# Layer 0 of a two-layer convolution kernel: large transfers cut into parts that are issued in successive groups

## The chip, the cores and the metric

The kernel runs on one core of a Trainium2 chip. The metric is the time of one execution on the device in microseconds (us). Engines are named as in the profile: PE (matrix multiplications; PEld is its loading of weights), DVE, ACT and POOL (vector, activation and general engine), and SP, which here only issues transfers (DMAs). ACT and POOL can issue transfers too.

## The reference

The input x has 4 images of 16 channels and 256 x 256 pixels. Two layers follow each other; each adds to x a function of the group-normalized x (8 groups of 2 channels).

```python
# layer 0: 25 logits per channel from a 3x3 convolution, softmax over them,
# weighted sum of the 5x5 neighbourhood of the normalized input
out = conv3x3(gn(x), conv_w) + conv_b              # 16 * 25 outputs per pixel
weights = softmax(out.reshape(N, C, 25, H, W), axis=2)
x = x + einsum('ncuij,ncuij->ncij', unfold5x5(gn(x)), weights)
# layer 1: silu and 8 cubic B-spline bases of each 3x3 patch, two small contractions
out = einsum('bjhwn,ijn->bihw', silu(patches), base_w)
out = out + einsum('bjhwns,ijns->bihw', bspl, spl_w) + bias
x = x + out
```

## The kernel before

A short start computes the statistics of x and prepares the weights. Then `layer0` computes the first layer, and `layer1` the second; layer 1 begins when layer 0's last strips are done.

**Strips and groups.** Layer 0 goes over 64 strips: 4 images (`b`), 2 halves of 128 rows (`hf`, the rows lie on the partitions), 8 strips of 32 columns (`s`). A strip has 8 groups of `JG` = 4 columns, so layer 0 has 512 groups. For one group PE multiplies, for each of the 4 columns, a piece of the tile `am` (L922) and of the tile `an` (L926) with the weights, which gives the 400 logits `lg` (in PSUM, three buffers). ACT takes their exponential into `e` (L945, two instructions per group, four buffers of `e`). POOL multiplies `e` with the 5x5 neighbourhood `u` (L950). DVE sums numerator and denominator into `nd` (L771). At the end of a strip ACT and DVE divide (L785 to L799), and POOL subtracts the result from the columns of `xc` (L805).

**What is loaded.** The tiles `am` and `an` hold the transposed columns of the normalized input for 8 columns, two groups, from the arrays `hst` and `hsl` in HBM. `load_im` issues three DMAs for `am` (L719) and two for `an` (L729), 779 KB together, two such periods ahead, into three buffers. `load_u` issues five DMAs of 288 KB (L743) for the next strip in the middle of a strip (column 16). `load_xc` issues one of 1 MB (L749), every fourth strip, for the four strips that come two strips later: `xc` holds 128 columns of x for all 16 channels. When the four strips have been subtracted, `xc` is x1, the result of layer 0, and `store` (L862) writes it twice into the array `x1s` for layer 1: two DMAs of 1 MB, issued by ACT, 15 times. The last one, the sixteenth, is issued by POOL.

**The next image.** While an image is computed, the generator `normalize` prepares the next one, one step per group: it loads rows `xp` (L315), ACT normalizes them into `hsp` and `ht`, `hsp` is stored (`put_rows`, L323), PE transposes `ht`, ACT copies the result into `tt` and `hi` (L393), DVE computes the remainder `lo` (L414), and `put_columns` (L337) stores the three tiles for both halves: six DMAs of 260 KB. The list `moves` holds what is due after a number of groups.

**What sets the order.** The program is written out as one sequence, and `in_order` makes each engine keep the order of that sequence. Within a group the sequence is: `load_im` (every second group), `load_u` and `load_xc` (at column 16), the matrix multiplications and exponentials, POOL's product, DVE's sum of the group before, then `step()`, then one step of `normalize`. `after(k, f)` puts `f` in the list `later`; `step()` runs what is due and counts the rest down, so `f` comes in the k-th group after. POOL's subtraction calls `after(1 + g, statistics, ...)` for the eight channel groups g and `after(2, store, n, xc)`; the store thus comes in group 0 of the strip two further than the last of the four.

SP, ACT and POOL each issue their transfers in their own order. The framework adds the waits: a transfer waits for the buffer it fills to be free, for the data it reads, and, since it announces its landing through one of a small number of semaphores that are used in turn, for the transfer that used that semaphore before. The turn runs through the transfers of SP and ACT together.

Of the kernel before, what the change touches and what calls it, by code (L numbers as in the profile page):

```python
# [34 lines left out]
def conv_preact_kernel(  # L35
# [12 lines left out]
    nc = tc.nc  # L48
    B, C, H, W = x.shape
    G = 8  # L50
    GC = C // G
    P = 128
    NH = H // P
    K = 5
# [7 lines left out]
    SW = 32  # L62
# [3 lines left out]
    CX = 128  # L66
# [4 lines left out]
    QC = 4  # L71
# [36 lines left out]
    for k, d in enumerate((0, RD - 1)):  # L108
        h = k * (P // 2)
# [148 lines left out]
    def zeros(b, queue):  # L258

        for e in (0, HP - PAD):  # L260
            for r in range(PAD):
                yield partial(
                    queue.dma_start,
                    hs[b][:, e + r].rearrange("s c w -> c s w"),
                    zero[0:C, 0 : NST * SP].rearrange("c (s w) -> c s w", s=NST),
                )
        yield partial(
            queue.dma_start,
            bass.AP(
                tensor=x1s[b].tensor, offset=x1s[b].offset,  # L270
                ap=[[CP, C], [(H + 1) * W, 2], [1, W]],
            ),
            zero[0 : 2 * C, 0:W],
        )
        for h in range(NH):
            for w in (0, (W + 1) * RP):
                yield partial(queue.dma_start, hst[b][h][:, w : w + RP], zero[0:C, 0:RP])
                yield partial(
                    queue.dma_start,
                    hsl[b][h][:, :, w : w + RP].rearrange("c t r -> (c t) r"), zero[:, 0:RP],  # L280
                )
# [8 lines left out]
    def normalize(b, ptr, tiles, held=None, copier=None, part=None, dense=False):  # L290
# [5 lines left out]
        prep, xps, tts, his, los = tiles  # L296
        copier = copier or nc.scalar.copy

        moves = [(20 + 4 * i, f) for i, f in enumerate(zeros(b, nc.sync))]
        moves = moves if held is None and part is None else []  # L300
# [25 lines left out]
                hsp.rearrange("p s c w -> p s (c w)"),  # L326
            )

        def put_columns(q, n):
            g0 = n * QG  # L330
            for h in parts:

                for to, ti, t in ((hst, 0, tts[n]), (hsl, 0, his[n]), (hsl, 1, los[n])):
                    d = to[b][h]
                    m = 2 if to is hsl else 1
                    t = t if t.dtype == F32 else t.bitcast(F32)
                    nc.sync.dma_start(  # L337
                        bass.AP(
                            tensor=d.tensor,
                            offset=d.offset + q * QC * m * CT + ti * CT + (1 + g0) * RP,  # L340
                            ap=[[QW * RP, W // QW], [m * CT, QC], [1, QG * RP]],
                        ),
                        t[:, h].rearrange("p g r -> p (g r)"),
                    )
# [41 lines left out]
        def columns(q, n, h):  # L386

            tp = ptr.tile([P, QG, P], F32, name=f"tp{b}_{q}_{n}_{h}", tag="tp")

            def copy(t, to, keep):  # L390

                if h in parts:
                    to(t[:, h, :, 1 : 1 + P], tp)  # L393
                if part == 1:
                    to(t[:, 1, :, 0:1], keep[:, q * NQ + n])
                elif h == 1:
                    to(t[:, 0, :, RP - 1 :], tp[:, :, 0:1])
                else:
                    to(t[:, 1, :, 0:1] if part is None else keep[:, q * NQ + n], tp[:, :, P - 1 :])

            for k in range(QG):
                nc.tensor.transpose(
                    tp[:, k, :], hts[q, h][:, n * QG + k].rearrange("p w c -> p (w c)"), ident
                )
            if not dense:
                yield
            copy(tts[n], copier, kept[0])
            copy(his[n], nc.scalar.copy, kept[1])
            if not dense:
                yield  # L410

            v = slice(1, 1 + P) if h in parts else slice(RP - 1, RP)
            to = h if h in parts else 0
            nc.vector.tensor_sub(  # L414
                los[n][:, to, :, v], tp[:, :, 0 : v.stop - v.start],
                his[n][:, to, :, v].bitcast(F32),
            )
            if part == 0 and h == 0:
                moves.append((1, partial(
                    nc.scalar.copy, kept[2][:, q * NQ + n], los[n][:, 0, :, P : P + 1]  # L420
                )))
            if part == 1:
                nc.scalar.copy(los[n][:, 1, :, 0:1], kept[2][:, q * NQ + n])
            if h == NH - 1:
                if part is None:
                    moves.append((5, partial(border, los[n])))
                moves.append((9 if part is None else 4, partial(put_columns, q, n)))
            yield
            yield
            yield  # L430
            yield
# [28 lines left out]
    with tc.tile_pool(name="prep0", bufs=2) as prep, tc.tile_pool(  # L460
# [24 lines left out]
        for dj in range(3):  # L485
            v = conv_wt[dj].rearrange("(d c) n -> c d n", d=3)
# [5 lines left out]
        v = conv_wt[2, 2 * C : 3 * C]  # L492
# [10 lines left out]
        for d in range(3):  # L503
# [3 lines left out]
            v = spl_s[dc]  # L507
# [89 lines left out]
        for b in range(B):  # L597
            st = stat.tile([P, G, NH * (GC if b == 0 else 1), 6], F32, name=f"st0_{b}", tag=f"st0{min(b, 1)}")
            for hf in range(NH):
                n = b * NH + hf  # L600
                t = loaded.pop(0)
# [27 lines left out]
            ms = stat.tile([P, 2], F32, name=f"ms_{b}", tag="ms")  # L629
# [5 lines left out]
            v = hm[:, b * NH : (b + 1) * NH]  # L635
# [46 lines left out]
    def newest(engine):  # L682
        return [i for i in nc.cur_bb.bb.instructions if i.engine == engine][-1]
# [7 lines left out]
    def layer0(shift):  # L691
# [4 lines left out]
        with tc.tile_pool(name=f"prep{arm}", bufs=2) as prep, tc.tile_pool(  # L696
# [38 lines left out]
                    )  # L735
                return am, an

            def load_u(n):
                b, hf, s = strips[n]
                u = l0.tile([P, K, C, SP], F32, name=f"u_{n}{arm}", tag="u")  # L740
                for m in range(K):
                    r0 = hf * P + m
                    nc.sync.dma_start(u[:, m], hs[b][s, r0 : r0 + P])  # L743
                return u

            def load_xc(n):
                b, hf, s = strips[n]
                xc = x1p.tile([P, C, CX], F32, name=f"xc_{n}{arm}", tag="xc")
                nc.sync.dma_start(  # L749
                    xc, x[b, :, hf * P : (hf + 1) * P, s * SW : s * SW + CX].rearrange(  # L750
                        "c p w -> p c w")
                )
                return xc

            waiting, later, seeds = [], [], []

            def after(k, f, *args):

                later.append([k, partial(f, *args)])
# [36 lines left out]
            def quotient(n, nd, xc, r):  # L798
                nc.vector.tensor_mul(nd[:, 1], nd[:, 1], r)  # L799
                after(LAG + 2, apply, n, nd, xc)  # L800

            def apply(n, nd, xc):
                w0 = strips[n][2] * SW % CX
                v = xc[:, :, w0 : w0 + SW]
                nc.gpsimd.tensor_sub(v, v, nd[:, 1])  # L805
                seeds[1:] = [newest(POOLE)]
                if w0 + SW == CX:
                    if n == len(strips) - 1:
                        store(n, xc)
                        after(1, last_statistics, n, xc)  # L810
                    else:
                        for g in range(G):
                            after(1 + g, statistics, n, xc, g)
                        after(2, store, n, xc)

            def columns_of(n):
                b, hf, s = strips[n]
# [34 lines left out]
                add(vz, vz, mz)  # L852
                nc.gpsimd.tensor_scalar(st1[b][:, 1, :, k], vz, float(GC * CX), None, ALU.mult)

            def store(n, xc):
                b, hf, s = strips[n]
                c0 = s * SW + SW - CX
                v = x1s[b][:, W : W + H * W].rearrange("c (p w) -> p c w", w=W)

                queue = nc.gpsimd if n == len(strips) - 1 else nc.scalar  # L860
                for h in range(2):
                    queue.dma_start(  # L862
                        v[hf * P : (hf + 1) * P, h * C : (h + 1) * C, c0 : c0 + CX], xc
                    )


            nc.scalar.add_instruction(
# [5 lines left out]
                )  # L873
            )
            ims = [load_im(0)]
            us = [load_u(0)]
            ims.append(load_im(1))
            nxc, xc = load_xc(0), None
            ahead = iter(())
            for n, (b, hf, s) in enumerate(strips):  # L880
                if (hf, s) == (0, 0):
# [17 lines left out]
                u = us.pop(0)  # L899
                if s * SW % CX == 0:  # L900
                    xc = nxc

                nd = ndp.tile([P, 2, C, SW], F32, name=f"nd_{n}{arm}", tag="nd")
                for j in range(0, SW, JG):
                    if j % CI == 0:
                        k = n * nci + j // CI
# [5 lines left out]
                    if j == SW // 2:  # L912
                        if n + 1 < len(strips):
                            us.append(load_u(n + 1))
                        if s * SW % CX == 2 * SW and n + 2 < len(strips):
                            nxc = load_xc(n + 2)
                    e = l0.tile([P, 2, JG, K, C, K], F32, name=f"e_{n}_{j}{arm}", tag="e", bufs=LAG + 3)
                    for j1 in range(0, JG, 2):
# [12 lines left out]
                        if shift:  # L931
                            mx = l0.tile([P, 2, C], F32, name=f"mx_{n}_{j}_{j1}{arm}", tag="mx")
                            for i in range(2):
                                v = lg[:, i, :NL].rearrange("p (m c d) -> p m c d", m=K, c=C)
# [404 lines left out]
    with tc.If(fast > 0) as small_logits:  # L1339
        layer1("", *layer0(False))  # L1340
# [44 lines left out]
```

## Time and profile before

| | |
|---|---|
| median of 3 runs | 2912.49 us (2910.01 to 2913.32) |
| the profiled execution | 2906.7 us, its span 2904.9 us |
| busy share of the span: PE, DVE, ACT, POOL | 93%, 96%, 73%, 93% |
| moved by the DMAs | 664.43 MB, mean 229 GB/s |
| layer 0, first to last L771 | 123.8 to 2028.5 us |
| L950 on POOL, L771 on DVE, mean of one | 3.547 us, 3.477 us |

A row of the profile names line, engine, operation, and tiles as out<-in; then, after the bar, busy us in total and mean ns of one; then the idle time of the engine just before such instructions and which instruction's end ended it. Back-to-back instructions overlap by about 0.08 us. A row with SPq or ACTq is of the engine's issuing part: the second number is the time of issuing, not of the transfer. A view of waits has, for each pair, the total us, how many waits, and the longest.

### The profile page before, as it was taken

What the parts mean: (1) busy time and instruction counts of PE and PEld (TensorE: products, weight loads), DVE (VectorE), ACT (ScalarE), POOL (GpSimd) and SP (SyncE); (2) the same over time, 40 slices, a digit from 0 to 9 for tenths busy, and PEclk for the clock granted to TensorE, in tenths of its full rate; (3) what the DMA queues carried; (4) which work ended last, traced back from release to release, by engine and by line L of the source; (5) the groups of instructions that cost most, each with busy time, mean ns of one, the idle gap of its engine ahead of it and who ended that gap; (6) DMA issues with size and microseconds to landing.
All of it is one profiled execution on the core that took longest, in us unless ns stands there. A gap on an engine that the chain in (4) does not pass through costs nothing.

```text
span 2904.9 us, 40991 instructions
## 1 busy us (share of the span) xinstructions
PE 2715.8 (93%) x14282; PEld 1499.0 (52%) x14282; DVE 2803.1 (96%) x1866; ACT 2126.4 (73%) x2764; POOL 2704.7 (93%) x1117
## 2 busy tenths in 40 slices
PE   4699999999999999999999999997799999999998
PEld 3466656666666656656656656664233343333222
DVE  7599999999999999999999999999899999999996
ACT  6566876667757567676655655557899999999995
POOL 4399999999999999999999999999899999999995
PEclk7799999999999999999999999999899999999999
DMA  9988999879889688888976767765788888787883
GB/s 284 263 236 233 253 257 268 238 212 248 237 229 259 190 223 232 236 245 229 249 205 178 189 168 196 186 177 177 248 250 251 250 248 257 239 265 241 254 250 100
DMA packets 403467, 664.43 MB, mean 229 GB/s; under 512 B 43186, under 2 KB 267908, under 8 KB 387380
## 3 DMA queue, kind: packets, MB, share of 16 engines
q1 hardware_dynamic: 339284, 626.53, 76.5%
q10 hardware_dynamic: 61920, 31.46, 3.8%
q0 software_dynamic: 2048, 3.72, 0.4%
q8 instruction: 117, 1.92, 0.3%
q14 instruction: 98, 0.80, 0.1%
HBM read 532.96 MB, written 121.15 MB: 225 GB/s over the span
## 4 chain that ended last, share of the span: by engine, by line
DVE 49%; PE 27%; DMA 7%; ACT 6%; issue 5%; POOL 3%; SPq 2%; DVEq 0%; ACTq 0%; POOLq 0%
DVE nd L771 39%; PE yp L1252 12%; PE lg L922 10%; PE yp L1261 3%; PE lg L926 3%; DVE ring L175 3%; DVE s L172 2%; DMA an<-hsl 2%; POOL e L950 2%; DMA x1s<-xc 1%; DMA xin<-in_x_dram 1%; DVE r1a L1096 1%; ACT xtb L1087 1%; DVE nd L799 1%; DVE r L795 1%
## 5 line engine op out<-in xcount | busy, mean ns | idle before, releaser
L950 POOL TENSOR_TENSOR e<-e,u 128x1600 f32<-128x1600 f32 x512 | 1789.0, 3547 | 48.9 <-ACT e L945 32.4
L922 PE MATMUL lg<-wm,am 128*128 128x400 f32 x4096 | 1736.9, 505 | 69.8 <-ACT e L945 37.5
L771 DVE TENSOR_REDUCE nd<-e 128x128 f32<-128x3200 f32 x512 | 1758.6, 3477 | 29.7 <-POOL e L950 29.3
L926 PE MATMUL lg<-wn,an 97*128 97x400 f32 x2048 | 1346.9, 658 | 15.2 <-DMA an<-hsl 15.2
L945 ACT ACTIVATE e<-lg 128x800 f32<-128x800 f32 x1024 | 835.3, 839 | 578.2 <-PE lg L926 337.8
L922 PEld LDWEIGHTS lg<-wm,am 128*128 128x128 f32 x4096 | 764.9, 193 | 383.0 <-ACT e L945 69.1
L1252 PE MATMUL yp<-ring,wt 128*32 128x512 f32 x6144 | 722.2, 595 | 35.4 <-DVE ring L175 34.8
L926 PEld LDWEIGHTS lg<-wn,an 97*128 97x128 f32 x2048 | 389.0, 190 | 334.3 <-DMA an<-hsl 23.6
L1252 PEld LDWEIGHTS yp<-ring,wt 128*32 128x32 f32 x6144 | 228.8, 109 | 494.5 <-issue 404.3
L1109 POOL TENSOR_TENSOR s1b<-s1b,r1a 128x1024 f32<-128x1024 f32 (+1 forms) x96 | 192.7, 2038 | 0.0
L1109 POOL TENSOR_TENSOR s1a<-s1a,r1a 128x1024 f32<-128x1024 f32 (+1 forms) x96 | 192.0, 2031 | 0.0
L825 ACT ACTIVATE z<-xc,nrm 128x256 f32<-128x256 f32 x240 | 144.0, 600 | 17.5 <-POOL xc L805 13.5
L175 DVE SCALAR_TENSOR_TENSOR ring<-s,s1a 128x1024 f32<-128x1024 f32 x132 | 154.9, 1193 | 0.9
L175 DVE SCALAR_TENSOR_TENSOR ring<-s,s1b 128x1024 f32<-128x1024 f32 (+1 forms) x128 | 152.0, 1208 | 0.3
L1109 POOL TENSOR_TENSOR s1a<-s1a,r1b 128x512 f32<-128x512 f32 (+2 forms) x68 | 119.3, 1778 | 0.0
L1109 POOL TENSOR_TENSOR s1b<-s1b,r1b 128x512 f32<-128x512 f32 x64 | 114.8, 1819 | 0.0
L1105 POOL TENSOR_TENSOR s1a<-r1b 128x1536 f32<-128x1536 f32 (+1 forms) x31 | 86.6, 2793 | 27.9 <-ACT r1b L1094 27.9
L172 DVE SCALAR_TENSOR_TENSOR s<-xta,cb,s 128x1024 f32<-128x1024 f32 (+2 forms) x90 | 111.3, 1257 | 0.3 <-DMA sla<-x1s 0.2
L172 DVE SCALAR_TENSOR_TENSOR s<-xtb,cb,s 128x1024 f32<-128x1024 f32 (+2 forms) x85 | 106.0, 1268 | 3.7 <-ACT s L169 3.7
L172 DVE SCALAR_TENSOR_TENSOR s<-xtc,cb,s 128x1024 f32<-128x1024 f32 (+2 forms) x85 | 105.9, 1268 | 0.0
L169 ACT ACTIVATE s<-xta,cb 128x1024 f32<-128x1024 f32 (+2 forms) x90 | 96.4, 1085 | 12.4 <-DVE ring L175 10.8
L1105 POOL TENSOR_TENSOR s1b<-r1b 128x1536 f32<-128x1536 f32 (+1 forms) x32 | 86.3, 2697 | 18.5 <-ACT r1b L1094 18.5
(209 smaller groups left out, 2300.0 us busy)
## 6 DMA issues: line engine op xcount, KB each, us to landing
am<-hst SPq DMA_DIRECT2D x512, 194.6 KB
u<-hs SPq DMA_DIRECT2D x320, 288.0 KB
an<-hsl SPq DMA_DIRECT2D x512, 129.8 KB
xta<-x1s SPq DMA_DIRECT2D x40, 1024.0 KB
xtb<-x1s SPq DMA_DIRECT2D x40, 1024.0 KB
xtc<-x1s SPq DMA_DIRECT2D x40, 1024.0 KB
am<-hst SPq DMA_DIRECT2D x256, 129.8 KB
x1s<-xc ACTq DMA_DIRECT2D x30, 1024.0 KB
```

The source lines that it names most:

```text
L169: nc.scalar.activation(s, t, AF.Square, scale=-0.5, bias=cb)
L172: nc.vector.scalar_tensor_tensor(p, t, cb2, s, ALU.subtract, ALU.mult)
L175: nc.vector.scalar_tensor_tensor(f, p, 0.0, q, ALU.min, op)
L771: nc.vector.tensor_reduce(nd[:, :, :, j : j + JG].rearrange("p t c j -> p t j c"), e.rearrange("p t j m c d -> p t j c m d"), AX.XY, ALU.add,)
L825: nc.scalar.activation(z, v, f, scale=nrm[b][:, 0, g : g + 1], bias=nrm[b][:, 1, g : g + 1], accum_out=st1[b][:, t, g, columns_of(n) : col ...
L922: nc.tensor.matmul(lg[:, i, :NL], lhsT=am[:, o : o + P], rhs=wm.rearrange("p m c d -> p (m c d)"), start=True, stop=False,)
L926: nc.tensor.matmul(lg[:, i, :NL], lhsT=an[:, o : o + P], rhs=wn.rearrange("p m c d -> p (m c d)"), start=False, stop=True,)
L945: nc.scalar.activation(ev, lg[:, :, :NL], AF.Exp)
L950: nc.gpsimd.tensor_tensor(e[:, 1].rearrange("p j m c d -> p j (m c) d"), e[:, 0].rearrange("p j m c d -> p j (m c) d"), uv, ALU.mult,)
L1105: nc.gpsimd.tensor_tensor(s1(n, a, z), r1(n, a, z), r1(n, a, z), ALU.mult)
L1109: nc.gpsimd.tensor_tensor(s1(n, a, z), s1(n, a, z), r1(n, a, z), ALU.mult)
L1252: nc.tensor.matmul(yp[t * M : (t + 1) * M], lhsT=wt[:, d, e].rearrange("p r o -> p (r o)"), rhs=ring[:, r0 + t * RT + d : r0 + t * RT + d ...
```

## The change

Three transfers are cut or spread:

- `store_in_pieces` replaces the call of `store`, except for the last xc: four parts of 4 channels for each of the two copies, eight DMAs of 256 KB, one in each of eight successive groups (counts 2 to 9 instead of 2).
- `load_xc` issues four DMAs of 4 channels, the first at once and the others after 0, 1 and 2 groups. `load_u` issues two of its five at once, two after 0 groups and one after 1. The first loads of layer 0 stay as they were.
- `put_columns` of the next image stores `tt` after 5 moves, `hi` after 7, `lo` after 9, two DMAs each, instead of all six after 9. The preparation of image 0 stays as it was.

```diff
-                moves.append((9 if part is None else 4, partial(put_columns, q, n)))
+                if part is None:
+                    for i in range(3):
+                        moves.append((5 + 2 * i, partial(put_columns, q, n, (i,))))
+                else:
+                    moves.append((4, partial(put_columns, q, n)))
...
-                for m in range(K):
-                    r0 = hf * P + m
-                    nc.sync.dma_start(u[:, m], hs[b][s, r0 : r0 + P])
+                def rows(*ms):
+                    for m in ms:
+                        r0 = hf * P + m
+                        nc.sync.dma_start(u[:, m], hs[b][s, r0 : r0 + P])
+
+                if not spread:
+                    rows(*range(K))
+                else:
+                    rows(0, 1)
+                    after(0, rows, 2, 3)
+                    after(1, rows, 4)
...
-                nc.sync.dma_start(
-                    xc, x[b, :, hf * P : (hf + 1) * P, s * SW : s * SW + CX].rearrange(
-                        "c p w -> p c w")
-                )
+                for i, c in enumerate(range(0, C, QC)):
+                    part = partial(
+                        nc.sync.dma_start,
+                        xc[:, c : c + QC],
+                        x[
+                            b, c : c + QC, hf * P : (hf + 1) * P, s * SW : s * SW + CX
+                        ].rearrange("c p w -> p c w"),
+                    )
+                    if i == 0 or not spread:
+                        part()
+                    else:
+                        after(i - 1, part)
...
-                        after(2, store, n, xc)
+                        store_in_pieces(2, n, xc)
...
+            def store_in_pieces(k, n, xc):
+                for i, c in enumerate(range(0, C, QC)):
+                    for h in range(2):
+                        after(k + 2 * i + h, store, n, xc, [(h, slice(c, c + QC))])
```

`store` takes the list of pieces and issues one DMA for each, with the queue and the target as before.

More of the change, by code (lines that the diff above doesn't have):

```diff
@@ L327, in put_rows, with put_columns @@
             )
-        def put_columns(q, n):
+        def put_columns(q, n, which=(0, 1, 2)):
             g0 = n * QG
             for h in parts:
-                for to, ti, t in ((hst, 0, tts[n]), (hsl, 0, his[n]), (hsl, 1, los[n])):
+                sides = ((hst, 0, tts[n]), (hsl, 0, his[n]), (hsl, 1, los[n]))
+                for to, ti, t in (sides[i] for i in which):
                     d = to[b][h]
@@ L736, in load_im, with load_u, load_xc @@
                 return am, an
-            def load_u(n):
+            def load_u(n, spread=True):
                 b, hf, s = strips[n]
                 u = l0.tile([P, K, C, SP], F32, name=f"u_{n}{arm}", tag="u")
-                for m in range(K):
-                    r0 = hf * P + m
-                    nc.sync.dma_start(u[:, m], hs[b][s, r0 : r0 + P])
+                def rows(*ms):
[8 more added lines that the diff above has]
+                    after(1, rows, 4)
                 return u
-            def load_xc(n):
+            def load_xc(n, spread=True):
                 b, hf, s = strips[n]
                 xc = x1p.tile([P, C, CX], F32, name=f"xc_{n}{arm}", tag="xc")
-                nc.sync.dma_start(
-                    xc, x[b, :, hf * P : (hf + 1) * P, s * SW : s * SW + CX].rearrange(
-                        "c p w -> p c w")
-                )
+                for i, c in enumerate(range(0, C, QC)):
[10 more added lines that the diff above has]
+                        after(i - 1, part)
                 return xc
@@ L853, in last_statistics, with store @@
                 nc.gpsimd.tensor_scalar(st1[b][:, 1, :, k], vz, float(GC * CX), None, ALU.mult)
-            def store(n, xc):
+            def store(n, xc, pieces=None):
                 b, hf, s = strips[n]
@@ L860, in store @@
                 queue = nc.gpsimd if n == len(strips) - 1 else nc.scalar
-                for h in range(2):
+                for h, c in pieces or [(h, slice(0, C)) for h in range(2)]:
                     queue.dma_start(
-                        v[hf * P : (hf + 1) * P, h * C : (h + 1) * C, c0 : c0 + CX], xc
-                    )
+                        v[hf * P : (hf + 1) * P, h * C + c.start : h * C + c.stop, c0 : c0 + CX],
+                        xc[:, c],
+                    )
+            def store_in_pieces(k, n, xc):
+                for i, c in enumerate(range(0, C, QC)):
+                    for h in range(2):
+                        after(k + 2 * i + h, store, n, xc, [(h, slice(c, c + QC))])
             nc.scalar.add_instruction(
@@ L875, in layer0 @@
             ims = [load_im(0)]
-            us = [load_u(0)]
+            us = [load_u(0, False)]
             ims.append(load_im(1))
-            nxc, xc = load_xc(0), None
+            nxc, xc = load_xc(0, False), None
             ahead = iter(())
```

## The prediction

> **What bounds the kernel now.** I read the busy shares first, then the table by windows of 100 us, then the waits of the issuing queue SP, then one store close up. Strips and groups are counted from 0; (30,4) is group 4 of strip 30.
>
> ```profile
> DVE  7599999999999999999999999999899999999996
> ...
> POOL 4399999999999999999999999999899999999995
> ...
> L950 POOL TENSOR_TENSOR e<-e,u 128x1600 f32<-128x1600 f32 x512 | 1789.0, 3547 | 48.9 <-ACT e L945 32.4
> ...
> L771 DVE TENSOR_REDUCE nd<-e 128x128 f32<-128x3200 f32 x512 | 1758.6, 3477 | 29.7 <-POOL e L950 29.3
> ```
>
> Layer 0 runs from 123.8 us (first L771) to 2028.5 us: 3.72 us for each of its 512 groups. DVE has no spare time there: an L771 per group plus, per strip, three divisions of 0.68 and some subtractions L414 of the same length. Its idle time before L771 is all that faster data could give back: 29.3 us, in 15 waits. By windows, 15.6 of it is the start (120 to 140 us) and 4.9 lies at 1680 to 1735, where the scales for layer 1 are made; neither holds a transfer that the change touches. The other 8.8 us are 0.7 (410 to 450), 2.4 (790 to 840), 1.9 (1010 to 1050), 1.6 (1260 to 1315) and 2.2 (1480 to 1525): each stretch follows a store of x1. 8.8 us, 0.30% of the span, is the most that this change can win, with at most 1 us more in waits too short to be listed.
>
> Why a store stalls anything is in SP's own waits:
>
> ```profile
> SPq L719 <- PE lg L926: 483.1, 175, 5.7
> ...
> SPq L729 <- DMA x1s<-xc: 74.7, 10, 14.6
> SPq L719 <- DMA x1s<-xc: 67.1, 17, 10.9
> ...
> SPq L337 <- DMA x1s<-xc: 24.1, 2, 12.2
> ```
>
> Normally SP waits for PE to free an im buffer. But it spends 74.7 + 67.1 + 24.1 + 7.5 (L323) = 173 us waiting for stores that ACT issues, 11.6 us for each of 15 pairs, though no load needs their data. The built order with its waits says why: the transfers of SP and ACT take eight completion semaphores in turn, and a transfer waits until the one eight places before it has landed. A store on ACT holds a place in that row, and SP stands still until ACT has come to it and it has landed. One pair close up, from the timelines of ACT, SP, PE, POOL and DVE:
>
> ```profile
> 1011.05 2.19 ACTq L862 DMA_DIRECT2D x1s<-xc  x2
> ...
> 1003.78 0.52 SPq L337 DMA_DIRECT2D hsl<-lo  x1
> 1016.26 0.52 SPq L337 DMA_DIRECT2D hst<-tt  x1
> ...
> 1019.13 0.65 PE L926 MATMUL lg<-wn,an 97*128 97x400 f32 x1
> 1025.43 1.67 PE L922 MATMUL lg<-wm,am 128*128 128x400 f32 x2 [5.65 <-ACT r L787]
> ...
> 1031.94 7.01 POOL L950 TENSOR_TENSOR e<-e,u 128x1600 f32<-128x1600 f32 x2 [4.80 <-ACT e L945]
> ...
> 1035.48 3.49 DVE L771 TENSOR_REDUCE nd<-e 128x128 f32<-128x3200 f32 x1 [1.17 <-POOL e L950]
> ...
> 1043.70 3.49 DVE L771 TENSOR_REDUCE nd<-e 128x128 f32<-128x3200 f32 x1 [0.73 <-POOL e L950]
> ```
>
> SP issues nothing from 1004.3 to 1016.26, which is 5.2 us after ACT began its first store. The am load behind it goes out at 1019.95 to 1021.81 (three issues, 1.86), and PE restarts at 1025.43, 3.6 us after the last. PE idles 5.65 us and then loses about 2 more on slower matmuls (columns 1.91, 1.66 and 0.97 apart, 0.86 before); DVE loses 1.17 + 0.73. So the buffers lg and e absorb some 5.7 us of PE's lateness.
>
> **What the Trainium skill says.** *DMA: Bandwidth & Descriptors*, "Anatomy of one DMA": "any semaphore wait happens on the issuing sequencer before dispatch". The trace agrees: the 12.0 us gap stops every later transfer of SP. *Perfetto Trace Analysis*, "Summary: the profiler window per engine type": a hardware DMA's row shows its issue, not the data's movement. Here too: the pair's row is 2.19 us, while SP is released 5.2 us after its start. *DMA: Bandwidth & Descriptors*, "Rules for kernel authors", wants 1 MiB or more per transfer and small ones joined. That speaks against quarters; the trace of before has no 256 KB store, so it is a bound below and not a number.
>
> **The change part by part.** PE, DVE and POOL keep the same instructions in the same order in the built programs, so everything goes through SP, ACT and the semaphores.
>
> *Loads of u and xc.* Same five issues of u, four of xc for one. They are put after later groups, but SP moves on without waiting for groups: in the built order the five u rows and three xc parts still follow each other ahead of the next am load, which alone waits for PE. Only the last quarter of xc falls behind that load. Three more issues of about 0.4 us, 14 times, lie inside SP's 483 us of waiting for PE. Cost and gain 0, bounds -1 to +1; if that cover goes they add to the lateness below.
>
> *Stores of columns.* Still six of 260 KB, now in pairs two groups apart, and so with an am/an load between. That is real spreading. It removes part of what is seen at 790 to 840 and 1260 to 1315, where six puts, u and xc follow each other; that is inside the 8.8. No new wait: tt goes five groups after its copies, lo as late as before.
>
> *Stores of x1.* Two of 1 MB become eight of 256 KB on ACT, one per group (0 to 7 of the strip). Issue: before 2.19 us; after, 8 x 0.37 (a first store's share) = 3.0 us, spread over eight groups, on an engine that is 52 to 77% busy in these windows: 0. Each quarter also waits for the transfer eight places before it. Behind that wait stand ACT's activations L945, and PE waits for those; but eight places back is a load of one or two groups earlier, landed by then if SP is on time, so I take 0, with up to 1 us per store if SP is late. What goes is the 5.2 us of landing behind each pair, and so up to 8.8 us on DVE. What comes is that SP now depends on ACT's progress in eight successive groups. For the pair of before the first load behind the stop is the one for (x,4), three groups of PE after the store. For the eighth quarter of after, issued in (x,7), the built order puts that stop in front of, or at most three issues ahead of, the am load that PE needs at (x+1,2): two groups later.
>
> The ledger, counted from the end of PE's group 0 for before, 7 for after. Strip 30 before: 1.5 to ACT's store (1009.5 to 1011.05), 5.2 landing, 5.55 of issues to the last am (three puts of columns in front), 3.6 landing = 15.9; PE wants it at 3 x 3.43 = 10.3; late 5.6, and 5.65 is seen. After: 1.5, then a quarter's landing, 1.86, 3.6, against 2 x 3.43 = 6.9. The quarter's landing is the unknown. Landings listed in the chain of waits are 3.6 to 3.8 at the fast end (am, an, 130 to 195 KB) and 5.3 to 6.2 at the slow end; the 1 MB store took 5.2. I take 3.6 (bounds 3.2 and 5.2): 10.6, late 3.7, and with the 2 us of slow matmuls 5.7. That is just what the buffers absorb: DVE loses 0. In six of the 15 stores one to three more issues (0.5 each) stand between; those lose 0.5 to 1.5, about 6 us in all. The last rows of u also come behind late quarters, and POOL wants them at (x+1,0); mostly within its own lead, so counted in the same 6.
>
> Sum: -8.8 + 6 = -3 us, so the profiled 2904.9 (2906.7 with what lies around the span) becomes about 2902. The median of the runs shown is 2912.5, 5.8 above the profiled execution; I subtract the same 3: 2909.5. Layer 1 keeps its order, its loads too.
>
> **The rivals.**
> *All stalls go (faster).* Quarters land in 3.2 us, or SP had more lead: nothing is lost and -8.8 remains: about 2903.5. For it: each quarter is a fourth of the bytes, and SP is no longer shut out for 12 us at once. Against: the ledger leaves no margin at (x+1,2), and earlier quarters hold SP too.
> *SP is held by ACT for eight groups (slower).* If a quarter lands in 4.5 us, each store costs 0.9 more, 15 x 0.9 = 13.5, beside the 6: +10.7, about 2923; at 5.2 us 15 x 1.6 + 6 - 8.8 = +21, about 2933.5. It decides from a landing of about 3.8, where 15 times the excess over 3.6 plus 6 reaches 8.8. For it: loads in the chain often take over 5 us. Against: quarters meet less traffic than the 2 MB burst.
> *The spread is none.* SP's loads keep their clump and the old stalls return under other names: 0, about 2912.5.
>
> **How the numbers follow.** A measurement of this kernel can tell about 0.2% (5.8 us) from no change. Even trade, -3, with the rival of no spread: 0.38. All stalls go, counting cases in which the new losses stay under 3 us: 0.37. Held SP: 0.25. The even trade's own range is 2906 to 2917. For 8 in 10 I go to all stalls gone plus 1 us of short waits and the runs' own scatter, 2900, and to a quarter landing in about 4.8 us, 2927.
>
> **What would show it.** Right: waits of SP for x1s stores more in number but each under some 6 us; PE's waits for am no longer before (x,4) but before (x+1,2); DVE's idle before L771 falls from 29.3 to about 26. Wrong: DVE idle near 20.5 (first rival) or above 35 (second), PE or POOL then waiting for am, an or u at the start of the strip after each store; or any change in layer 1, after 2034 us.

## The result and the profile after

The changed kernel takes **2934.43 us** (median of 4 runs, 2931.64 to 2937.41) against 2912.90 us before (4 runs, 2910.01 to 2915.34): ratio 1.0077, 95% interval 1.0065 to 1.0090. It is 0.77% slower. The forecast was 2909.5 with a range of 2900 to 2927, so it missed on the high side. The rival "SP is held by ACT for eight groups" had named 2933.5.

The profiled execution took 2935.1 us, its span is 2933.2 us, 28.3 more than the profiled one of before. First the lines of the page that answer to those shown of before: the busy tenths of DVE and POOL, and the costliest groups (busy us, mean ns of one, then the idle time ahead of them and what ended most of it).

```profile
DVE  6599999999999999999999999999899999999997
...
POOL 4399998999999999999999999999899999999995
...
L976 POOL TENSOR_TENSOR e<-e,u 128x1600 f32<-128x1600 f32 x512 | 1789.4, 3544 | 79.0 <-ACT e L971 60.8
L948 PE MATMUL lg<-wm,am 128*128 128x400 f32 x4096 | 1749.1, 508 | 99.8 <-DMA am<-hst 77.6
L791 DVE TENSOR_REDUCE nd<-e 128x128 f32<-128x3200 f32 x512 | 1762.7, 3480 | 55.8 <-POOL e L976 54.8
```

The work itself is unchanged: a POOL product lasts 3544 ns (3547 before), a DVE reduction 3480 (3477). What grew is idle time. DVE waits 54.8 us for POOL, 29.3 before: 25.5 of the 28.3 us. POOL waits 60.8 for ACT (32.4 before), and PE 77.6 for `am` (18.3 before, from the view of waits):

```profile
PE lg L922 <- DMA am<-hst: 18.3, 10, 5.2
```

The row of PE tells the origin: data. The tenths are too coarse to show it.

Where it lies tells the view of DVE's waits, cut so that the start and the making of the scales for layer 1 stay out: 160 to 1680 us before, 160 to 1730 us now.

```profile
DVE nd L771 <- POOL e L950: 8.8, 10, 2.1
```
```profile
DVE nd L791 <- POOL e L976: 29.6, 24, 3.2
```

Now 2.9 us more follow the scales, after the store in strip 54. The waits behind stores have thus grown from 8.8 to 32.5 us; 1.9 us more came at the start of layer 0, which has no store.

Layer 1 is as it was (876.4 us from the last reduction of layer 0 to the end before, 874.0 now). SP's waits for stores of x1, line by line, total us, number and longest:

```profile
SPq L724 <- PE lg L952: 384.0, 165, 4.8
...
SPq L724 <- DMA x1s<-xc: 90.0, 29, 6.8
SPq L734 <- DMA x1s<-xc: 79.8, 22, 12.1
SPq L750 <- DMA x1s<-xc: 67.8, 19, 6.7
...
SPq L338 <- DMA x1s<-xc: 23.5, 5, 8.6
...
SPq L787 <- DMA x1s<-xc: 15.6, 6, 5.6
SPq L772 <- DMA x1s<-xc: 15.1, 6, 8.6
SPq L323 <- DMA x1s<-xc: 15.0, 3, 8.8
```

The sum is 306.8 us in 90 waits; before it was 173.4 in 30. Each wait is shorter, 3.4 us rather than 5.8, but there are three times as many. And 98.5 us of it now stand at L750, L772 and L787, the loads of u and xc. What that does is seen close up at the store in strip 18. (It stores strips 12 to 15: POOL's last subtraction for them comes while PE is in strip 18. A store thus begins three strips after its last strip, not two as the text on the order has it.) The lines are from the timelines of ACT, SP, PE, POOL and DVE (start us, duration, row, and in brackets the idle time before it and what ended it):

```profile
686.70 0.42 ACTq L882 DMA_DIRECT2D x1s<-xc  x1
...
688.11 0.37 ACTq L882 DMA_DIRECT2D x1s<-xc  x1
...
686.76 0.43 SPq L787 DMA_DIRECT2D xc<-in_x_dram  x1
692.90 0.32 SPq L750 DMA_DIRECT2D u<-hs  x1
693.27 0.43 SPq L787 DMA_DIRECT2D xc<-in_x_dram  x1
693.74 0.50 SPq L306 DMA_DIRECT2D hs<-zero  x1
694.35 0.37 SPq L323 DMA_DIRECT2D hs<-hsp  x1
695.13 2.75 SPq L724 DMA_DIRECT2D am<-hst  x3
...
701.72 1.67 PE L948 MATMUL lg<-wm,am 128*128 128x400 f32 x2 [6.79 <-DMA am<-hst]
...
708.42 7.01 POOL L976 TENSOR_TENSOR e<-e,u 128x1600 f32<-128x1600 f32 x2 [4.07 <-ACT e L971]
...
711.99 6.97 DVE L791 TENSOR_REDUCE nd<-e 128x128 f32<-128x3200 f32 x2 [1.77 <-POOL e L976]
```

The first two rows are the seventh and the eighth quarter. SP issues nothing from 687.2 to 692.9. Then, before the `am` load that PE needs at (19,2), it still has to issue a row of u, a part of xc and two transfers of the next image. PE stands for 6.8 us, POOL for 4.1, DVE for 1.8 (and 0.3 at 719.28). This repeats after all 15 stores. With x for the strip in which a store begins, and counted by the L952 rows, four to a group, PE's long stop is before (x+1,2) each time. It is 6.2 us in the median, from one L952 to the next, less the usual 0.86; this takes in the first column after the stop, which is slow. The chain of waits passes through these stops. Two of its pieces in this stretch, the landing of the seventh quarter, which ends SP's long stop at 692.9, and then the landing of `am`:

```profile
686.70 6.18 DMA x1s<-xc
697.26 4.33 DMA am<-hst
```

### The profile page after: what moved, and what is told of

Read it like the earlier page. It is cut to its first block, busy times and chain, and to the rows that moved or that the text cites. A ratio compares the mean times of both kernels' runs of the same rounds, so it can differ in the third digit from the quotient of the medians.

```text
span 2933.2 us, 41139 instructions
## 1 busy us (share of the span) xinstructions
PE 2726.7 (93%) x14282; PEld 1517.7 (52%) x14282; DVE 2806.9 (96%) x1866; ACT 2131.6 (73%) x2764; POOL 2705.2 (92%) x1117
## 4 chain that ended last, share of the span: by engine, by line
DVE 35%; PE 34%; DMA 11%; ACT 7%; issue 6%; POOL 4%; SPq 2%; DVEq 0%; POOLq 0%; ACTq 0%
DVE nd L791 24%; PE lg L948 18%; PE yp L1278 9%; PE lg L952 5%; POOL e L976 3%; DVE ring L175 3%; DVE s L172 3%; DMA am<-hst 3%; DMA x1s<-xc 2%; PE yp L1287 2%; ACT xtc L1113 1%; DMA xin<-in_x_dram 1%; DVE r1a L1122 1%; ACT e L971 1%; DMA an<-hsl 1%
## 5 line engine op out<-in xcount | busy, mean ns | idle before, releaser
L976 POOL TENSOR_TENSOR e<-e,u 128x1600 f32<-128x1600 f32 x512 | 1789.4, 3544 | 79.0 <-ACT e L971 60.8
L948 PE MATMUL lg<-wm,am 128*128 128x400 f32 x4096 | 1749.1, 508 | 99.8 <-DMA am<-hst 77.6
L791 DVE TENSOR_REDUCE nd<-e 128x128 f32<-128x3200 f32 x512 | 1762.7, 3480 | 55.8 <-POOL e L976 54.8
L952 PE MATMUL lg<-wn,an 97*128 97x400 f32 x2048 | 1354.2, 661 | 8.9 <-DMA an<-hsl 8.5
L971 ACT ACTIVATE e<-lg 128x800 f32<-128x800 f32 x1024 | 845.7, 840 | 652.2 <-PE lg L952 570.5
L948 PEld LDWEIGHTS lg<-wm,am 128*128 128x128 f32 x4096 | 773.1, 194 | 407.3 <-issue 97.2
L952 PEld LDWEIGHTS lg<-wn,an 97*128 97x128 f32 x2048 | 391.3, 191 | 332.8 <-issue 20.4
```

Source lines behind the costliest of these rows:

```text
L791: nc.vector.tensor_reduce(nd[:, :, :, j : j + JG].rearrange("p t c j -> p t j c"), e.rearrange("p t j m c d -> p t j c m d"), AX.XY, ALU.add,)
L948: nc.tensor.matmul(lg[:, i, :NL], lhsT=am[:, o : o + P], rhs=wm.rearrange("p m c d -> p (m c d)"), start=True, stop=False,)
L952: nc.tensor.matmul(lg[:, i, :NL], lhsT=an[:, o : o + P], rhs=wn.rearrange("p m c d -> p (m c d)"), start=False, stop=True,)
L971: nc.scalar.activation(ev, lg[:, :, :NL], AF.Exp)
L976: nc.gpsimd.tensor_tensor(e[:, 1].rearrange("p j m c d -> p j (m c) d"), e[:, 0].rearrange("p j m c d -> p j (m c) d"), uv, ALU.mult,)
```

## The experiments

Each time below is a median, beside the runs of the kernel before on the same chip (2909.8 to 2911.2 us). The ratio is to those, with its 95% interval. Differences between two experiments can be between two chips, so that 1 or 2 us of them mean nothing. "(x,0)" is the group in which the kernel before issues its stores.

### Which part of the change costs

**Stores of x1 alone** (the kernel before with this):

```diff
-                        after(2, store, n, xc)
+                        store_in_pieces(2, n, xc)
```

> The kernel before with one part of the change: x1 leaves as eight quarters in eight successive groups; u, xc and the columns are loaded and stored as before. Theory (the stop): the loss comes from the stops of SP behind late quarters, the last of them issued in (x,7), so this part alone brings nearly all of it: 2930 to 2938 us, DVE's idle time before its reduction 48 to 58 us, PE waiting for am before (x+1,2). Rival (crowding): the loss comes from the three more issues of each xc, and from u rows and xc parts standing between the stop and the load that PE needs; with one issue of xc instead of four it would be half or less: 2915 to 2924 us, DVE idle 32 to 42 us.

Measured: 2955.59 us, 1.0149 (1.0130 to 1.0167). The loss is in the stores, and alone they cost more than the whole change: 44.4 us. DVE waits 74.6 us for POOL, PE 89.8 for `am`. So the rest of the change gives back some 21 us; neither theory had said that.

**Loads and columns without the stores** (the changed kernel with this):

```diff
-                        store_in_pieces(2, n, xc)
+                        after(2, store, n, xc)
```

> The changed kernel with the x1 store put back to two transfers of 1 MB, both in (x,0); loads of u and xc in parts and columns in pairs stay. Theory (the stop): no late stop, so no loss: 2908 to 2914 us, DVE idle before its reduction 24 to 32 us. Rival (crowding): the parts of xc and u behind the store's stop cost by themselves: over 2918 us, DVE idle over 36 us.

Measured: 2901.63 us, 0.9967 (0.9955 to 0.9978): 9.6 us faster, better than both theories.

**Columns in pairs alone**, all else as before:

> The kernel before with the columns stored in three pairs, two groups apart, and nothing else of the change. Theory: the pairs take puts away from between the stop of a store and the am load at (x,4), which is where the 9.6 us of loads and columns together come from: 2900 to 2906 us. Rival (the gain comes from u and xc in parts): 2908 to 2914 us.

Measured: 2901.16 us, 0.9976 (0.9964 to 0.9988), 9.5 faster, in the range of the theory. DVE's wait for POOL is 24.2 us, 29.3 before.

**Loads of u and xc in parts alone**, all else as before:

> The kernel before with u and xc loaded in parts, and nothing else of the change. Theory (SP does not wait between the parts, so they are not spread): 2908 to 2914 us, as before. Rival (their parts really interleave with the im loads): 2900 to 2906 us.

Measured: 2903.09 us, 0.9981 (0.9974 to 0.9988), 7.6 faster. The rival's number came, but not its reason: the parts do help, although no am or an load goes between the five u rows and the first three xc parts, and SP issues one behind the other, with 0.9 us between two of them at most. The two gains don't add (9.5 and 7.6, together 9.6): both seem to relieve the same stalls, those behind the 1 MB stores. Where the gain of the loads arises is open. The profiled executions do not resolve it: with loads alone DVE's wait for POOL is 27.7 us, with loads and columns together 28.4.

### Size, number or place of the stores

**All eight quarters in one group**:

```diff
-                        after(k + 2 * i + h, store, n, xc, [(h, slice(c, c + QC))])
+                        after(k, store, n, xc, [(h, slice(c, c + QC))])
```

> The changed kernel, but all eight quarters of x1 are issued one behind the other in (x,0). Same transfers, same sizes, no spread. Theory (the stop): what matters is in which group the last store is issued, so this is like the kernel before, perhaps a little longer because ACT issues eight rather than two (3.0 us rather than 2.2) and every one waits for its place in the row of eight: 2909 to 2918 us, DVE idle 26 to 36 us. Rival (size): small transfers land more slowly per byte and delay the loads beside them, wherever they are put: 2930 to 2940 us.

Measured: 2927.67 us, 1.0058 (1.0039 to 1.0077). It is 26 us above the same loads and columns with two 1 MB stores, where the theory had expected little. But the rival's reason doesn't hold either. The waits of PE, and of SP at the issue of `an`:

```profile
PE lg L952 <- DMA an<-hsl: 61.4, 18, 6.0
...
SPq L734 <- DMA x1s<-xc: 178.2, 19, 19.0
```

PE now waits for `an`, in the first columns of (x,2), not for `am` before (x+1,2). Eight stores in a row fill the whole turn of eight semaphores, so SP's very next transfer is stopped. In the built order that is mostly an `an` load wanted one group after the store. Two stores leave six transfers of SP in between. Number matters here through place.

**Two halves of 1 MB, seven groups apart**:

```diff
-                for i, c in enumerate(range(0, C, QC)):
-                    for h in range(2):
-                        after(k + 2 * i + h, store, n, xc, [(h, slice(c, c + QC))])
+                for h in range(2):
+                    after(k + 7 * h, store, n, xc, [(h, slice(0, C))])
```

> The changed kernel, but x1 leaves as two transfers of 1 MB again, the first in (x,0), the second in (x,7), seven groups apart. Theory (the stop): one late stop is enough. It stands where the eighth quarter stood, and a 1 MB transfer lands later (5.2 us or more, against 3.7), so each store loses at least as much as with eight quarters: 2932 to 2950 us, DVE idle 52 to 70 us, PE waiting for am before (x+1,2). Rival (number of stops): it is the eight stops together that use up SP's lead, so two stops cost little: 2910 to 2918 us. Rival (size): large transfers as before, so as before: 2910 to 2914 us.

Measured: 2920.66 us, 1.0036 (1.0023 to 1.0050), 19 us above both halves in (x,0). The theory's place is right (PE waits 62.1 us for `am`, 56.9 of it before (x+1,2)), its size too large.

```profile
PE lg L947 <- DMA am<-hst: 62.1, 19, 5.8
```

The 1 MB transfer in (x,7) landed after 5.1 us in the median; the eighth quarter of the changed kernel, at the same place, after 5.6. So one late stop costs more than half of the loss, and cutting to 256 KB did not make that stop shorter.

**Two halves of 1 MB, three groups apart** (`k + 3 * h` in place of `k + 7 * h`):

> As the halves seven groups apart, but the second 1 MB goes in (x,3) instead of (x,7). The order of SP's transfers says that its stop then stands ahead of at most five issues, none of them u or xc, of a load wanted two to four groups later. Theory (what stands between the stop and PE's need: groups of PE's work, less the u rows and xc parts queued ahead of the am load): the loss of the halves seven apart (19 us against both in one group) is gone: 2897 to 2906 us, DVE idle before its reduction 22 to 32 us. Rival (every separate stop costs): half the loss stays: 2910 to 2920 us.

Measured: 2909.94 us, 0.9999 (0.9990 to 1.0008). It lies between the two theories. 11 of the 19 us are gone, 8 stay. PE still waits 33.6 us for `am`, 24.8 of it before (x+1,2), with stops of up to 5.3 us. Why two separate stops of 1 MB cost 8 us is open.

**Eight quarters, two in each of four groups** (`k + i` in place of `k + 2 * i + h`):

> The changed kernel with the same eight quarters from ACT, but two in each of the groups (x,0) to (x,3) instead of one in each of (x,0) to (x,7). In SP's order most of their stops stand ahead of loads wanted three or four groups later, with no u or xc between; only at (22,2) does the order leave one group. Theory (place and clump): most of the loss goes: 2902 to 2914 us, no waits of PE for am before (x+1,2). Rival (every stop costs, wherever it is): eight stops, so near the changed kernel: 2922 to 2936 us.

Measured: 2903.41 us, 0.9980 (0.9974 to 0.9987). The waits of PE and DVE:

```profile
DVE nd L791 <- POOL e L976: 27.3, 9, 13.6
...
PE lg L948 <- DMA am<-hst: 24.9, 14, 4.3
```

The same eight quarters from the same engine, ended in (x,3) instead of (x,7), are 31 us faster than the changed kernel. Size and number alone are out as causes; it is the groups (x,4) to (x,7). The theory's "no waits" was too much: 10.6 of the 24.9 us are still before (x+1,2), 4.2 us at the longest.

### What stands between the last stop and the load

**u and xc loaded two groups earlier**:

```diff
-                    if j == SW // 2:
+                    if j == SW // 4:
```

> The changed kernel, with the loads of u and xc moved from group 4 of a strip to group 2. In SP's order the clump of u rows and xc parts then no longer stands between the stop of the last quarters and the am load that PE needs at (x+1,2), but in front of the load that it needs at (x+1,0), behind the quarters of (x,4) and (x,5). Theory (the stop with the clump behind it): PE's waits move from before (x+1,2) to before (x+1,0), most of all after strips 10, 22 and 38; the sum is somewhat smaller: 2918 to 2932 us. Rival (the last quarter alone, wherever the clump is): the waits stay before (x+1,2), and the time stays at 2930 to 2938 us.

Measured: 2943.97 us, 1.0106 (1.0090 to 1.0123). The sum is worse than expected, the place as expected. From PE's timeline, the stop after the store of strip 10:

```profile
455.99 1.67 PE L948 MATMUL lg<-wm,am 128*128 128x400 f32 x2 [9.07 <-DMA am<-hst]
```

By the count of L952 rows this is before (11,0). All long stops behind stores moved there from (x+1,2), the longest after strips 10, 14, 38 and 22.

**u and xc loaded two groups later** (`j == 3 * SW // 4`):

> The changed kernel with the loads of u and xc moved from group 4 of a strip to group 6, behind the am load for (x+1,2). Theory (the clump of u and xc between the last stops and that am load is what the ledger left out): the stop of (x,7) now stands behind that load, ahead of u: PE's waits for am before (x+1,2) go from 77 us to under 30, but the last u rows come late for POOL at (x+1,0), which shows as waits of POOL for u: 2910 to 2935 us, by which of the two is larger. Rival (the eight stops hold SP anyway): PE's waits for am stay at 60 us or more.

Measured: 2974.55 us, 1.0220 (1.0203 to 1.0237). From the waits:

```profile
DVE nd L791 <- POOL e L976: 94.2, 33, 13.5
...
PE lg L948 <- DMA am<-hst: 56.2, 19, 5.9
...
POOL e L976 <- DMA u<-hs: 24.7, 6, 9.9
```

No long stop before (x+1,2) is left; PE's waits for `am` are still 56.2 us (under 30 was expected), but before (x,4) and (x+1,4), where the clump now stands in front. And POOL waits for u, as expected, only more. In both runs the stall goes where the u rows and xc parts go: the stop delays all that is queued behind it, and what is wanted first behind it stalls. The move alone does not do it: in strips other than x and x+1, whose loads have no store ahead of them, PE has no stop over 1.5 us at the places to which the stalls moved.

### Who issues the store

**SP issues the eight quarters**:

```diff
-                queue = nc.gpsimd if n == len(strips) - 1 else nc.scalar
+                queue = nc.gpsimd if n == len(strips) - 1 else nc.sync
```

> The changed kernel, with the eight quarters issued by SP instead of ACT, in the same eight groups. ACT then issues no transfers there, so no place in the row of eight is held by an engine other than SP. Theory (the stop: SP waits for ACT's progress): no load waits for ACT any more; the loss is gone and the stalls of the kernel before too: 2890 to 2903 us, DVE idle 18 to 28 us, SP's waits for x1s stores nearly none. Rival (crowding: the small writes slow the loads beside them, whoever issues them): 2920 us or more, DVE idle over 40 us.

Measured: 2897.14 us, 0.9954 (0.9938 to 0.9971), 37 us faster than with ACT. PE, DVE and POOL keep the order of their instructions. The waits:

```profile
POOL e L976 <- ACT e L971: 37.9, 32, 12.1
...
DVE nd L791 <- POOL e L976: 21.3, 5, 13.1
```

The view of DVE's waits from 160 to 1700 us lists no wait for POOL at all. SP's waits for x1 stores are 3.4 us in sum, in 10 waits. SP instead waits 579.4 us for PE at L724 (384.0 with ACT), which is the spare time that it should have.

**SP issues two of 1 MB** (the same word, stores as before, loads and columns in parts):

> The changed kernel with x1 stored as two transfers of 1 MB in (x,0), as before, but issued by SP; loads and columns in parts. Theory (the stop): as with quarters on SP, no dependence on ACT: 2890 to 2905 us. Rival (size: in one queue a load lands behind 2 MB of stores, 5 to 10 us late by the landings of before): PE waits for am behind each store and it is 2910 to 2930 us; then the cut into quarters has a use, once it is on SP.

Measured: 2894.63 us, 0.9944 (0.9927 to 0.9960). The rival is out: 2 MB in SP's own queue don't hold the loads back enough to be seen. Against the quarters it is 2.5 us less, under what can be told apart. So the cut has no use on SP. The Trainium skill, *DMA: Bandwidth & Descriptors*, "Rules for kernel authors", asks for 1 MiB or more per transfer for the most bandwidth; for this kernel the size made no measurable difference on SP.

**The kernel before with SP issuing**, nothing else of the change:

> The kernel before, with one word changed: x1 is stored by SP rather than by ACT, as two transfers of 1 MB in (x,0); loads and columns as before. Theory: all stalls behind stores come from SP's wait for ACT, so this alone gives what the SP version with loads and columns in parts gave: 2893 to 2899 us. Rival (the row of six column puts also delays the loads, with or without a stop): 2900 to 2906 us.

Measured: 2894.67 us, 0.9950 (0.9934 to 0.9967): 16 us faster than the kernel before and 40 faster than the changed one, by one word. Loads and columns in parts add nothing on top (2894.63). They only eased what the stops did.

```profile
DVE nd L771 <- POOL e L950: 22.9, 6, 13.1
```

**POOL issues the eight quarters** (`queue = nc.gpsimd`):

> The changed kernel with the eight quarters issued by POOL in the same groups. POOL's transfers take other semaphores than the eight of SP and ACT, so SP has no stop; but they are a second queue beside SP's, as ACT's are. Theory (SP's stop): no waits of SP for x1s stores and no waits of PE for am before (x+1,2); what POOL's issuing costs shows as POOL's own time, some 1 us a piece at most 120 us in all, of which little is free: 2895 to 2925 us. Rival (two queues share the DMA engines, and the stores push the loads back): PE's waits for am before (x+1,2) stay, 70 us or more in all, 2930 us or more.

Measured: 2967.99 us, 1.0197 (1.0180 to 1.0214). The time missed the theory's range, but the mechanism is clear. SP has no wait for an x1 store, PE none for `am`. Instead, from the view of the tile x1s (min, median and max ns) and from the waits:

```profile
L882 POOL DMA_DIRECT2D x1s<-xc x122: 791/793/1217, 301.7 to 2102.7; - x122
```
```profile
DVE nd L791 <- POOL e L976: 84.3, 91, 13.0
```

120 issues of 0.79 us are 95 us of POOL, which has hardly any to spare, and DVE waits 63 us more than with SP. The stores are a second queue here as they are from ACT, and they land no sooner (5.3 us in the median; 3.7 from ACT), and yet no load came late: that a second queue takes the DMA engines from the loads is not the cause. In the traces SP and ACT use the same eight completion semaphores, and POOL eight others, as the theory needs. A kernel in which ACT issues the stores with semaphores of their own was not built, so for ACT's queue this is inferred from POOL's.

**POOL issues two of 1 MB**:

> The changed kernel with x1 stored by POOL as two transfers of 1 MB in (x,0). A fourth of the issues on POOL. Theory (SP's stop): no stop, little of POOL's time: 2893 to 2903 us, as with SP issuing. Rival (two queues compete): 1 MB from a second queue holds the loads back for 5 to 10 us as in the kernel with ACT issuing: 2901 us or more and PE waiting for am at (x,4).

Measured: 2910.09 us, 1.0001 (0.9992 to 1.0009). The time lies in the rival's range, but not for its reason: PE waits 4.8 us for `am`, so hardly a load is held. It is 15.5 us over SP as the issuer: 30 more issues on POOL, 24 us of it at the 0.79 us of a quarter, and DVE's wait for POOL is 33.5 us, 12 more than with SP. On POOL the cut into quarters costs 58 us; its 90 more issues of 0.79 us are 71 us of POOL.

The Trainium skill, *DMA: Bandwidth & Descriptors*, "Issuing engines are not separate DMA queues", says that issuing from several engines at once saves only the time of issuing on the sequencer, which is usually little beside the transfer. No run here measures that by itself. The runs add a case in which the choice of the engine decides: 37 us between ACT and SP for the quarters, and 16 for the pair of 1 MB in the kernel before, through a wait that the shared semaphores put on SP's sequencer.

## Why the prediction was wrong

**What bounds the kernel, and where a loss would show: right.** DVE has no spare time, so its idle time before the reduction is the measure: 25.5 of the 28.3 us. The place was named to the group: PE before (x+1,2), after every store. The mechanism was named as well, as the second rival. That its 2933.5 meets the measured 2934.4 is in part luck: it took a landing of 5.2 us, and left the other terms below as they were.

**Old stalls go: right in kind.** SP's single waits became shorter and more, the longest spacing of PE's columns at a stop before (x,4) went from 7.7 to 3.0 us. And 8.8 us on DVE was about the whole of what can be won there: with SP issuing, all of it is gone. The medians gain 16 us. About 6 of that don't show between the profiled executions, since the one of before lies 4 us below the median of its runs and the one with SP issuing 2.5 above. The runs of before scatter over 2904 to 2918, those with SP issuing over 2892 to 2898.

**The step that failed is the ledger of the eighth quarter.** Its terms, counted from PE's end of (x,7), beside the median of the 15 stores in the trace of the changed kernel:

| term | predicted | measured |
|---|---|---|
| ACT issues the eighth quarter | 1.5 | 0.0 |
| it lands | 3.6 (3.2 to 5.2) | 5.6 |
| SP's last long stop ends | 5.1 | 5.2 |
| from there to the end of the last `am` issue | 1.86 | 2.8 (mean 3.0) |
| landing of `am` | 3.6 | 3.8 |
| sum | 10.6 | 11.9 |
| PE wants it at | 6.9 | 6.9 |
| late | 3.7 | 5.0 |

(In the column "measured" the medians don't add up, and the stop ends before the eighth quarter has landed: in 8 of the 15 stores it is the seventh, issued 1.4 to 4.7 us before, whose landing ends SP's last long stop.)

Two terms failed. The *landing* was taken from the fast end of the loads, and is 5.6 rather than 3.6; by luck this hardly shows in the sum, because ACT reached the eighth quarter 1.5 us earlier than the pair of before, and because of the seventh. The *issues* were taken as the three of `am`, with one to three more in six of the stores. The trace shows five or more in 11 of the 15, since u rows and xc parts stand there. That is 0.9 of the 1.3 us by which the sum moved. The runs with u and xc moved confirm that clump, the row of u and xc transfers, as the carrier.

**ACT at 0, layer 1 unchanged: right.** ACT's activations hardly wait for transfers in the changed kernel (1.6 and 0.6 us after x1 stores, in layer 0), and layer 1 is no longer than before.

**The balance had no margin.** The prediction let PE lose 5.7 us at each store, 3.7 of lateness and 2 of slow matmuls, and the buffers absorb just that. In the trace PE loses 7.5 us in the median, the stop and the slow columns after it. What `lg` and `e` absorb of it is no fixed 5.7 either: 5.3 us in the median, 3.8 to 7.0 (PE's loss less that of DVE). DVE loses 2.0 us on average behind a store, 30.5 of the 32.5 us above, where the prediction had 6; less the 8.8 of the old stalls, this is nearly all of what DVE lost more than before. A ledger that comes out exactly at the absorbing limit is no forecast of zero: every error upward is paid 15 times, and every error downward gains nothing. The second rival, with its price of 15 times the excess, deserved more than 0.25.

**Loads of u and xc at 0, columns inside the 8.8: too low.** Without the spread stores they gain 9.6 together, in the changed kernel some 21. SP doesn't wait between the parts, as said, as long as the stores are not spread; that this makes them worthless does not follow. In the changed kernel SP does wait between them, for the quarters (the 98.5 us above).

**The rival "The spread is none": wrong.** The pieces are spread, which is the trouble: the spread carries the stop into the groups in which u, xc and the next `am` are queued.

## What to carry to other kernels

A transfer on another engine's queue can stop the queue of the loads, though neither needs the other's data, when both take completion semaphores from one row, as SP and ACT do here: look for waits of the loading engine on stores. Before cutting such a store, let the loading engine issue it (16 us here, by one word); cutting and spreading makes more stops, and each delays everything queued between it and the next load that is wanted. Count those issues in the built order, and give a chain that ends at the limit of the buffers no credit for ending there.

## What the runs showed of the hardware

- A 256 KB quarter takes no fixed time to land. By its number in the store, the medians of the changed kernel are 2.3 us for the first, 3.3 to 4.6 for the second to seventh, 5.6 for the eighth, as long as 1 MB at the same place (5.1). The Trainium skill, *DMA: Bandwidth & Descriptors*, "Anatomy of one DMA", has for a DMA that gpsimd issues about 2.0 us plus the bytes at 436 GB/s, which gives an estimate of 2.6 us for 256 KB and 4.4 for 1 MB. The first quarter, though issued by ACT, is near it, the eighth is twice that. Issued by POOL, for which the page gives its figure, the quarters take 2.7 us at the least and 5.3 in the median. In these runs a landing belongs to its place in the traffic.
- Issuing costs the issuer very differently: a store takes 0.37 us of ACT's issuing part, beside its activations, and 0.79 us of POOL's own time.
- A stop of PE costs more than its length. After the 6.79 us at 701.72 the next columns came 2.02, 1.67 and 1.04 us apart instead of 0.86; the granted clock was 0.50 from 700 to 704 us and 0.78 from 704 to 708. The mean granted clock from 200 to 1900 us was 0.97 in the changed kernel and 1.00 with SP issuing.
